# Late residuals on VectorE, a block's last product ahead of the next turn, and a new order of stores in a graph-attention kernel

## The chip, the cores and the metric

The kernel runs on one core of a Trainium2 chip. The core has five engines that work side by side: TensorE (PE) multiplies matrices and transposes, VectorE (DVE) does elementwise work and reductions along a row, ScalarE (ACT) applies functions with a scale and a bias, GpSimd (POOL) does elementwise work in SBUF and issues gathers by index, and SyncE (SP) issues the other transfers. [...] Sixteen DMA engines move the data of all queues. The metric is the time of one execution on the device in microseconds, the lower the better.

## The reference

The computation is one graph-attention layer with a residual and a layer norm, for 4096 nodes with 512 features:

```python
def _L0_gnn_ref(h, adj_mat, W, a):
    ht = (h @ W).reshape(N, N_HEADS, N_HIDDEN).transpose(1, 0, 2)      # 4 heads of 512
    src = jnp.einsum('hnd,hd->hn', ht, a_src)
    dst = jnp.einsum('hnd,hd->hn', ht, a_dst)
    e = jax.nn.leaky_relu(src[:, :, None] + dst[:, None, :], SLOPE) + adj_mat[None]
    att = jax.nn.softmax(e, axis=-1)
    h_prime = jnp.einsum('hij,hjd->hid', att, ht)
    return h_prime.mean(axis=0)
x = _layernorm(x + _L0_gnn_ref(x, adj, L0_gnn_W, L0_gnn_a), axis=-1)
```

The adjacency matrix is 4096 by 4096 float32 (64 MB); its entries are zero or weights up to 1e9. With such weights added to the scores, the softmax of a row is as a rule one at its largest entry and zero elsewhere. The attention output of a row is then one row of x, times the mean of the four heads' weight matrices.

## The kernel before

The kernel uses that fact. For each of the 4096 rows it finds the largest adjacency entry, gathers that one row of x, multiplies it by the mean of the heads' weights, adds x, and normalises. It also proves for every row, with a bound on the scores, that the leading entry wins; rows that fail would be redone by a general branch (`general`, from line 529), which this input skips.

The 4096 rows are 32 blocks (`NB`) of 128 rows. Row `p * 32 + ib` of the matrix is row `p` of block `ib`, so a store of n neighbouring blocks writes n * 2 KB in one run for each of the 128 partitions. `hold` keeps x and later the output of all blocks in SBUF. `Q` is 4, `LATE` is 28 and `BEHIND` is 24. The blocks form three groups:

- Blocks 0 to 23: the residual is added on TensorE, as a product with the identity (`residual`, L221), into the accumulator in PSUM that the four products (`products`, L228) also write; ScalarE takes the statistics and finishes them (`stats`, `finish`) in the main loop. Their stores wait until the loads are queued.
- Blocks 24 to 27: x is not there yet when their products end. ScalarE sets the products aside in SBUF (`put_by`, L241), and x is added after the loop (`add_x`, L244), on GpSimd for 24 to 26 and on VectorE for 27.
- Blocks 28 to 31: x is loaded in time. The residual of 28 and 29 is an identity product on TensorE in the last round, that of 30 an addition on VectorE after its products (L511), and that of 31 two identity products of half a row each (`residual_in_halves`, L266). Most of these blocks take mean and variance on VectorE (`moments`, L281 and L285), the root on ScalarE (L287), the reciprocal (and, with `shift=True`, minus mean times reciprocal) on VectorE (`factor`, L290 and L292), and the ending on VectorE (`normalise`, L297) or ScalarE (`finish`, L261).

For each block the search has two levels. VectorE reduces the 4096 entries of a row to 128 maxima of 32 (`segment_maxima`, L163); `find_segment` takes the largest of them and its place, and GpSimd turns the place into an index and gathers the 32 entries of that segment from the adjacency matrix (L174, L176, L181). Two rounds later `find_column` finds the place within the segment, and GpSimd gathers the row of x (L198, L200, L186). For the last block, `find_column_in_row` searches all 4096 entries on VectorE instead (L206), so that it does not wait for the second gather. TensorE then turns the gathered block (`turn`, L213: four transposes, and a copy by ScalarE, L215) and multiplies.

The order is written out by hand: no scheduler moves anything, and what the main loop (`for t in range(NB)`) and the listing after it (lines 463 to 525) call in turn is each engine's own order. In the loop, round t searches block t, gathers x for block t - 2, multiplies for block t - 3, takes statistics of t - 4. From block 24 on, a block's last product waits until the next block's turn has been issued, so that the turn's copy runs beside it. After the loop come the endings of the last blocks, interleaved with the proof (`bound`, `test`, `count`, `report`).

SyncE issues all loads in the loop; the stores follow behind the last loads: two of four blocks (0 to 3, 4 to 7), eight of two (8 to 23), and at the end, in this order, blocks 28, 29, 24 with 25, 30, 26 with 27, and 31. A store is issued only when its blocks are finished, and those behind it in the list wait with it. Row gathers and segment gathers share GpSimd's queue, whose instructions also include the additions of `add_x` and the final factors of the blocks that ScalarE measures (`rstd`, L255 to L257).

Of the kernel before, what the change touches and what calls it, by code (L numbers as in the profile page):

```python
# [10 lines left out]
U32 = mybir.dt.uint32  # L11
# [55 lines left out]
def leading_rows(ctx, tc, x, adj, W, a, out, ident, v, n_bad, any_bad):  # L67
# [100 lines left out]
    def find_segment(ib):  # L168
        seg = seg_of.pop(ib)
        nc.vector.max(out=top[:, ib, :], in_=seg)  # L170
        at = small.tile([P, 8], U32, name="at")
        nc.vector.max_index(at, top[:, ib, :], seg)  # L172
        row = small.tile([P, 1], U32, name="row")
        nc.gpsimd.tensor_tensor(row, at[:, 0:1], first[:, ib : ib + 1], op=OP.add)  # L174
        lead = lead_pool.tile([P, E], F32, name="lead")
        nc.gpsimd.indirect_dma_start(  # L176
            out=lead, out_offset=None, in_=adj_segs,
            in_offset=bass.IndirectOffsetOnAxis(ap=row[:, :1], axis=0),
        )
        start = at_of[ib] = small.tile([P, 1], U32, name="start")  # L180
        nc.gpsimd.tensor_tensor(start, at[:, 0:1], width, op=OP.mult)  # L181
        lead_of[ib] = lead

# [33 lines left out]
    def residual(ib):  # L217
        start = ib not in o_ps
        if start:
            o_ps[ib] = psum.tile([P, D], F32, name="o")  # L220
        nc.tensor.matmul(o_ps[ib], ident, hold[:, ib, :], start=start, stop=False)  # L221
# [40 lines left out]

    def residual_in_halves(ib):
        o_ps[ib] = [psum.tile([P, D // 2], F32, name="o") for _ in range(2)]
        for k, o in enumerate(o_ps[ib]):
            nc.tensor.matmul(o, ident, hold[:, ib, ts(k, D // 2)], start=True, stop=False)  # L266
# [22 lines left out]
    def factor(ib, shift=False):  # L289
        nc.vector.reciprocal(rt[ib], rt[ib])  # L290
        if shift:
            nc.vector.scalar_tensor_tensor(  # L292
                nm[:, ib : ib + 1], mean_var[ib][:, 0:1], -1.0, rt[ib], op0=OP.mult, op1=OP.mult
            )
# [111 lines left out]
    COLUMN, PROJECT, STATS, FINISH = 2, 3, 4, 6  # L406

    for t in range(NB):
# [30 lines left out]
        if t == NB - 1:  # L439
            for late in range(LATE, NB):  # L440
                row_norm(late)
            residual(LATE)
            residual(LATE + 1)
# [21 lines left out]
    for ib in range(0, 2 * Q, Q):  # L465
        store(nc.sync, ib, Q)
    for ib in range(2 * Q, BEHIND, 2):
        store(nc.sync, ib, 2)
    find_column(NB - 2)
    add_x(nc.gpsimd, BEHIND)  # L470
    add_x(nc.gpsimd, BEHIND + 1)
    find_column_in_row(NB - 1)
    add_x(nc.gpsimd, BEHIND + 2)
    products(LATE, KB - 1, KB)
    residual_in_halves(NB - 1)
    turn(NB - 3)
    products(NB - 3, 0, KB - 1)
    moments(LATE)
    for ib in range(BEHIND, NB):
        find_inner(ib)  # L480
    bound(0)
    products(NB - 3, KB - 1, KB)
    stats(BEHIND)
    factor(LATE)
    normalise(LATE, o_ps.pop(LATE))
    bound(1)
    turn(NB - 2)
    bound(2)
    add_x(nc.vector, LATE - 1)
    stats(BEHIND + 1)  # L490
    moments(LATE - 1)
    products(NB - 2, 0, 2)
    bound(3)
    test()
    pg = count()
    products(NB - 2, 2, KB - 1)
    stats(BEHIND + 2)
    rstd(slice(BEHIND, BEHIND + 2))
    rstd(slice(BEHIND + 2, BEHIND + 3))
    moments(NB - 3)  # L500
    report(pg)
    turn(NB - 1)
# [4 lines left out]
    finish(BEHIND + 1)  # L507
    products(NB - 2, KB - 1, KB)
    products_of_half(NB - 1, 0)
    products_of_half(NB - 1, 1)  # L510
    nc.vector.tensor_add(hold[:, NB - 2, :], o_ps[NB - 2], hold[:, NB - 2, :])  # L511
    o_ps[NB - 2] = hold[:, NB - 2, :]
# [4 lines left out]
    finish(BEHIND + 2)  # L517
    finish(BEHIND + 3)
# [4 lines left out]
    for ib, n in ((NB - 4, 1), (NB - 3, 1), (BEHIND, 2), (NB - 2, 1), (BEHIND + 2, 2)):  # L523
        store(nc.sync, ib, n)
# [154 lines left out]
```

## Time and profile before

| quantity | value |
|---|---|
| median of 3 runs | 236.09 us (235.83 to 236.25) |
| the profiled execution's own time | 236.21 us |
| its span, first to last instruction | 234.6 us |
| granted TensorE clock, mean | 0.975 |
| busy: TensorE / VectorE / ScalarE / GpSimd | 83% / 80% / 48% / 43% |
| bytes moved by DMA | 97.21 MB, mean 414 GB/s |
| of these, read and written in HBM | 88.62 MB and 8.39 MB |
| SyncE's queue / GpSimd's queue | 88.08 MB / 8.92 MB |

The profile is one execution. A line of it names the engine, the line of the kernel, the operation, what it writes and reads, the count, the duration, and the idle time ahead of it with what ended that idle time. `L228` is line 228. A float32 product shows as two records on TensorE. The times in the lists of instructions are microseconds from the first instruction of the program. The DMA share is the mean over the 16 DMA engines.

### The profile page before, as it was taken

The page shows a single profiled execution, that of the slowest core. Times are in us where ns is not written, and L with a number is a line of the kernel's source. Part 1 is how long each engine was busy: PE and PEld are TensorE (multiplying, and loading weights), DVE is VectorE, ACT ScalarE, POOL GpSimd, SP SyncE. Part 2 cuts the span into 40 slices and gives each one's busy share as a digit, 9 for nine tenths or more (in the row PEclk, how much of TensorE's full clock was granted, in tenths as well). Part 3 has the DMA queues.
Part 4 walks back from the last instruction along what each step waited for, and adds up shares of the span by engine and source line. Part 5 has one row for each costly group of instructions (what it writes and reads, how often), then busy time and mean ns, then how long its engine had stood idle before and what let it go on. Part 6 is the DMA issues. An engine that isn't in the chain of part 4 may idle for free.

```text
span 234.6 us, 2498 instructions
## 1 busy us (share of the span) xinstructions
PE 195.2 (83%) x683; PEld 101.4 (43%) x683; DVE 188.4 (80%) x302; ACT 111.6 (48%) x267; POOL 101.2 (43%) x215
## 2 busy tenths in 40 slices
PE   0188929999999999999979879797998968698990
PEld 0034514756565655555534333242443423244460
DVE  1736875589869995999589989998799999989672
ACT  2012011255474747474758354646464645166582
POOL 1012232414527462646353645464365464549130
PEclk9999977999999999999999999999799999999998
DMA  6999999999999999999999999999999999999985
GB/s 226 439 428 426 443 425 430 415 440 412 440 420 426 424 437 434 425 424 428 427 432 433 425 433 422 432 418 429 425 432 418 422 425 427 411 425 419 417 355 210
DMA packets 13697, 97.21 MB, mean 414 GB/s; under 512 B 2152, under 2 KB 2664, under 8 KB 7792
## 3 DMA queue, kind: packets, MB, share of 16 engines
q1 hardware_dynamic: 10080, 88.08, 88.9%
q0 software_dynamic: 3584, 8.92, 9.6%
q8 instruction: 6, 0.10, 0.2%
q14 instruction: 11, 0.09, 0.1%
q10 hardware_dynamic: 16, 0.02, 0.0%
HBM read 88.62 MB, written 8.39 MB: 414 GB/s over the span
## 4 chain that ended last, share of the span: by engine, by line
DMA 45%; POOL 17%; issue 15%; PE 10%; DVE 9%; ACT 1%; POOLq 0%; SPq 0%; DVEq 0%
DMA adj_t<-in_adj_dram 42%; DVE seg L163 8%; PE o L228 7%; POOL lead L176 6%; POOL y L186 5%; DMA y<-in_x_dram,col 3%; POOL sd L256 2%; PE o L270 2%; POOL start L181 1%; POOL row L174 1%; POOL col L200 1%; PE tp L213 1%; PE o L221 1%; ACT yt L215 1%; POOL sd L255 1%
## 5 line engine op out<-in xcount | busy, mean ns | idle before, releaser
L163 DVE TENSOR_REDUCE seg<-adj_t 128x64 f32<-128x2048 f32 (+1 forms) x68 | 146.0, 2149 | 32.7 <-DMA adj_t<-in_adj_dram 32.3
L228 PE MATMUL o<-w_sum,yt 128*128 128x512 f32 x248 | 115.1, 605 | 1.7 <-ACT yt L215 1.7
L228 PEld LDWEIGHTS o<-w_sum,yt 128*128 128x128 f32 x248 | 44.5, 191 | 54.8 <-issue 42.3
L215 ACT COPY yt<-tp 128x512 f32<-128x512 f32 x32 | 18.8, 588 | 44.3 <-PE tp L213 44.3
L176 POOL DMA_INDIRECT lead<-in_adj_dram,row x32 | 32.3, 1010 | 15.5 <-POOL row L174 15.0
L186 POOL DMA_INDIRECT y<-in_x_dram,col x32 | 30.9, 965 | 15.4 <-POOL col L200 15.2
L318 PE MATMUL o<-hold,ident 128*128 128x512 f32 x32 | 18.9, 745 | 17.5 <-DMA hold<-in_L_gnn_W_dram 17.5
L213 PE MATMUL tp<-ident,y 128*128 128x128 f32 x128 | 20.0, 280 | 12.6 <-DMA y<-in_x_dram,col 12.6
L221 PE MATMUL o<-hold,ident 128*128 128x512 f32 x52 | 27.3, 611 | 0.0
L213 PEld LDWEIGHTS tp<-ident,y 128*128 128x128 f32 x128 | 14.9, 143 | 25.4 <-issue 25.0
L174 POOL TENSOR_TENSOR row<-at,first 128x1 uint32<-128x1 uint32 x32 | 6.1, 190 | 42.0 <-DVE at L172 42.0
L336 ACT COPY wt<-tp 128x512 f32<-128x512 f32 x16 | 9.2, 587 | 31.4 <-PE tp L334 31.4
L200 POOL TENSOR_TENSOR col<-start,within 128x1 uint32<-128x1 uint32 x31 | 5.9, 190 | 40.1 <-DVE within L198 40.1
L235 ACT ACTIVATE sq<-hold 128x512 f32<-128x512 f32 x32 | 19.8, 619 | 0.0
L342 PEld LDWEIGHTS pv<-at_d,wt 128*128 128x128 f32 x128 | 16.3, 191 | 6.8 <-ACT wt L336 4.0
L318 PEld LDWEIGHTS o<-hold,ident 128*128 128x128 f32 x32 | 7.4, 243 | 26.7 <-POOL row L174 11.0
L319 ACT ACTIVATE w_sum<-o 128x512 f32<-128x512 f32 x4 | 2.4, 598 | 33.9 <-PE o L318 33.9
L261 ACT ACTIVATE hold<-o,nm,sd 128x512 f32<-128x512 f32 x24 | 17.2, 771 | 0.0
L252 ACT ACTIVATE sq<-o,nm 128x512 f32<-128x512 f32 x24 | 16.5, 688 | 0.8
L342 PE MATMUL pv<-at_d,wt 128*128 128x2 f32 x128 | 15.3, 244 | 0.6 <-ACT wt L336 0.6
L250 ACT ACTIVATE sq<-o 128x512 f32<-128x512 f32 x24 | 14.6, 609 | 0.0
L334 PEld LDWEIGHTS tp<-ident,hold 128*128 128x128 f32 x64 | 7.9, 142 | 6.9 <-issue 6.9
(85 smaller groups left out, 139.8 us busy)
## 6 DMA issues: line engine op xcount, KB each, us to landing
adj_t<-in_adj_dram SPq DMA_DIRECT2D x27, 2048.0 KB, 31.3
hold<-in_x_dram SPq DMA_DIRECT2D x7, 1024.0 KB, 33.2
adj_t<-in_adj_dram SPq DMA_DIRECT2D x6, 1024.0 KB, 25.7
out_dram<-hold SPq DMA_DIRECT2D x10, 512.0 KB, 15.2
adj_t<-in_adj_dram SPq DMA_DIRECT2D x8, 512.0 KB
hold<-in_L_gnn_W_dram SPq DMA_DIRECT2D x4, 1024.0 KB
out_dram<-hold SPq DMA_DIRECT2D x2, 1024.0 KB
hold<-in_x_dram SPq DMA_DIRECT2D x2, 512.0 KB, 14.1
```

The lines of the kernel that those rows point to most:

```text
L163: nc.vector.tensor_reduce(seg_of[ib][:, ts(k, S // n)], adj_t[ib][:, ts(k, N // n)].rearrange("p (s e) -> p s e", e=E), axis=AX.X, op=OP.max,)
L176: nc.gpsimd.indirect_dma_start(out=lead, out_offset=None, in_=adj_segs, in_offset=bass.IndirectOffsetOnAxis(ap=row[:, :1], axis=0),)
L186: nc.gpsimd.indirect_dma_start(out=y, out_offset=None, in_=x, in_offset=bass.IndirectOffsetOnAxis(ap=col[:, :1], axis=0),)
L213: nc.tensor.transpose(tp[:, kb, :], y[:, ts(kb, P)], ident)
L215: nc.scalar.copy(yt, tp)
L221: nc.tensor.matmul(o_ps[ib], ident, hold[:, ib, :], start=start, stop=False)
L228: nc.tensor.matmul(o_ps[ib], yt_of[ib][:, kb, :], w_sum[:, kb, :], start=(start and kb == 0), stop=(kb == KB - 1),)
L235: nc.scalar.activation(sq, hold[:, ib, :], AF.Square, accum_out=xx[:, ib : ib + 1])
L252: nc.scalar.activation(sq, o, AF.Square, bias=nm[:, i], accum_out=sd[:, i])
L261: nc.scalar.activation(hold[:, ib, :], o_ps.pop(ib), AF.Identity, bias=nm[:, i], scale=sd[:, i])
L318: nc.tensor.matmul(o, ident, hold[:, w_at + kb * H + h, :], start=(h == 0), stop=(h == H - 1))
L342: nc.tensor.matmul(pv[:, kb, h : 2 * H : H], wt[:, k, :], at_d[:, k, h : 2 * H : H], start=(k == 0), stop=(k == KB - 1),)
```

## The change

Five edits, nearly all in what follows the last loads.

1. The identity products of blocks 28 and 29 are gone. Instead `add_residual` adds x on VectorE once the products are complete, as block 30 already had it; block 28's ending moves from VectorE to ScalarE, with the shift that it needs.
2. In `factor` the shift is a one-input operation with the reciprocal as a scalar, where it was a two-input operation.
3. Block 29's work is issued in another order: its turn now follows the last product of block 28 and stands ahead of block 31's residual halves; its own last product stands ahead of the turn of block 30, and three products of block 30 stand together ahead of the turn of 31, which comes before the moments of 29.
4. GpSimd: the second half of `find_segment` is a function of its own, `fetch_segment`; for block 31 it is called after block 30's row gather. Before block 31's row gather stands the addition of x for block 24 alone; those of 27, 25 and 26 follow it, 27's moved here from VectorE. The endings of 26 and 27 move from ScalarE to GpSimd (`finish_on_chip`).
5. SyncE: the stores of 0 to 23 go in the order `HELD`, with the two four-block stores third and sixth; the last six go as 28, 24 with 25, 26 with 27, 29, 30, 31.

```diff
     def find_segment(ib):
         seg = seg_of.pop(ib)
         nc.vector.max(out=top[:, ib, :], in_=seg)
-        at = small.tile([P, 8], U32, name="at")
+        at = at_of[ib] = small.tile([P, 8], U32, name="at")
         nc.vector.max_index(at, top[:, ib, :], seg)
+        if ib < NB - 1:
+            fetch_segment(ib)
+
+    def fetch_segment(ib):
+        at = at_of.pop(ib)
         row = small.tile([P, 1], U32, name="row")
...
-        start = at_of[ib] = small.tile([P, 1], U32, name="start")
-        nc.gpsimd.tensor_tensor(start, at[:, 0:1], width, op=OP.mult)
         lead_of[ib] = lead
+        if ib < NB - 1:
+            start = at_of[ib] = small.tile([P, 1], U32, name="start")
+            nc.gpsimd.tensor_tensor(start, at[:, 0:1], width, op=OP.mult)
...
+    def finish_on_chip(ib):
+        i, h = slice(ib, ib + 1), hold[:, ib, :]
+        o_ps.pop(ib)
+        nc.gpsimd.tensor_scalar(h, h, sd[:, i], nm[:, i], op0=OP.mult, op1=OP.add)
+
+    def add_residual(ib):
+        nc.vector.tensor_add(hold[:, ib, :], o_ps[ib], hold[:, ib, :])
+        o_ps[ib] = hold[:, ib, :]
...
         if shift:
-            nc.vector.scalar_tensor_tensor(
-                nm[:, ib : ib + 1], mean_var[ib][:, 0:1], -1.0, rt[ib], op0=OP.mult, op1=OP.mult
+            nc.vector.tensor_scalar(
+                nm[:, ib : ib + 1], mean_var[ib][:, 0:1], rt[ib], -1.0, op0=OP.mult, op1=OP.mult
             )
...
+    HELD = ((8, 2), (10, 2), (0, Q), (12, 2), (14, 2), (Q, Q), (16, 2), (18, 2), (20, 2), (22, 2))
...
                 row_norm(late)
-            residual(LATE)
-            residual(LATE + 1)
...
-    for ib in range(0, 2 * Q, Q):
-        store(nc.sync, ib, Q)
-    for ib in range(2 * Q, BEHIND, 2):
-        store(nc.sync, ib, 2)
+    for ib, n in HELD:
+        store(nc.sync, ib, n)
     find_column(NB - 2)
+    fetch_segment(NB - 1)
     add_x(nc.gpsimd, BEHIND)
-    add_x(nc.gpsimd, BEHIND + 1)
     find_column_in_row(NB - 1)
-    add_x(nc.gpsimd, BEHIND + 2)
+    for ib in (LATE - 1, BEHIND + 1, BEHIND + 2):
+        add_x(nc.gpsimd, ib)
     products(LATE, KB - 1, KB)
+    turn(NB - 3)
     residual_in_halves(NB - 1)
-    turn(NB - 3)
     products(NB - 3, 0, KB - 1)
+    bound(0)
+    stats(BEHIND)
+    add_residual(LATE)
     moments(LATE)
+    bound(1)
+    factor(LATE, shift=True)
     for ib in range(BEHIND, NB):
         find_inner(ib)
-    bound(0)
     products(NB - 3, KB - 1, KB)
-    stats(BEHIND)
-    factor(LATE)
-    normalise(LATE, o_ps.pop(LATE))
-    bound(1)
     turn(NB - 2)
+    finish(LATE)
+    moments(LATE - 1)
+    stats(BEHIND + 1)
     bound(2)
-    add_x(nc.vector, LATE - 1)
-    stats(BEHIND + 1)
-    moments(LATE - 1)
-    products(NB - 2, 0, 2)
     bound(3)
     test()
+    products(NB - 2, 0, KB - 1)
     pg = count()
-    products(NB - 2, 2, KB - 1)
     stats(BEHIND + 2)
     rstd(slice(BEHIND, BEHIND + 2))
     rstd(slice(BEHIND + 2, BEHIND + 3))
+    add_residual(NB - 3)
+    turn(NB - 1)
     moments(NB - 3)
     report(pg)
-    turn(NB - 1)
     factor(LATE - 1, shift=True)
     factor(NB - 3)
     normalise(NB - 3, o_ps.pop(NB - 3))
     finish(BEHIND)
     finish(BEHIND + 1)
+    finish_on_chip(BEHIND + 2)
+    finish_on_chip(BEHIND + 3)
     products(NB - 2, KB - 1, KB)
     products_of_half(NB - 1, 0)
     products_of_half(NB - 1, 1)
-    nc.vector.tensor_add(hold[:, NB - 2, :], o_ps[NB - 2], hold[:, NB - 2, :])
-    o_ps[NB - 2] = hold[:, NB - 2, :]
+    add_residual(NB - 2)
     moments(NB - 2)
     stats_of_half(NB - 1, 0)
     factor(NB - 2)
     normalise(NB - 2, o_ps.pop(NB - 2))
-    finish(BEHIND + 2)
-    finish(BEHIND + 3)
     stats_of_half(NB - 1, 1)
     moments(NB - 1)
     factor(NB - 1, shift=True)
     finish_in_halves(NB - 1)
-    for ib, n in ((NB - 4, 1), (NB - 3, 1), (BEHIND, 2), (NB - 2, 1), (BEHIND + 2, 2)):
+    for ib, n in ((LATE, 1), (BEHIND, 2), (BEHIND + 2, 2), (NB - 3, 1), (NB - 2, 1)):
         store(nc.sync, ib, n)
     store(nc.sync, NB - 1, 1)
```

## The prediction

> **What bounds the kernel now.** I read the page first, then the instructions in order of time for the last 35 us of each engine, then short stretches of the last 10 us for the DMA engines. All times below are on the profiled execution's clock: span 234.6 us, its own time 236.21 us, so 1.6 us lie outside the span; the median of the runs shown is 236.09 us, 0.12 us below it.
>
> The page's row of bytes a second (40 slices) and its sum:
>
> ```profile
> GB/s 226 439 428 426 443 425 430 415 440 412 440 420 426 424 437 434 425 424 428 427 432 433 425 433 422 432 418 429 425 432 418 422 425 427 411 425 419 417 355 210
> DMA packets 13697, 97.21 MB, mean 414 GB/s; under 512 B 2152, under 2 KB 2664, under 8 KB 7792
> ```
>
> From the second slice to the third from the end the 16 DMA engines are full. Nothing of the change touches the bytes. Only the last two slices (some 11.7 us) have room. In them TensorE is the busy engine. Its instructions in order of time:
>
> ```profile
> 203.58 0.63 PE L213 MATMUL tp<-ident,y 128*128 128x128 f32 x4 [1.84 <-DMA y<-in_x_dram,col]
> ...
> 207.61 1.88 PE L221 MATMUL o<-hold,ident 128*128 128x512 f32 x4
> ...
> 216.28 2.84 PE L228 MATMUL o<-w_sum,yt 128*128 128x512 f32 x6 [0.68 <-ACT yt L215]
> ...
> 221.21 1.99 PE L228 MATMUL o<-w_sum,yt 128*128 128x512 f32 x4 [0.37 <-ACT yt L215]
> ...
> 225.53 3.70 PE L270 MATMUL o<-w_sum,yt 128*128 128x256 f32 x16
> ```
>
> TensorE last waits for a gather at 203.58 and then runs to 229.2 with two holes, 0.68 and 0.37 us. Behind it stands block 31's ending, and then the last store:
>
> ```profile
> 229.27 0.43 DVE L304 BATCH_NORM_STATS2 halves_st<-o 128x6 f32<-128x256 f32 x1 [0.65 <-PE o L270]
> ...
> 230.69 0.56 ACT L310 ACTIVATE hold<-o,nm,sd 128x256 f32<-128x256 f32 x1 [0.42 <-DVE nm L292]
> ```
>
> So compute ends at 231.25, the last store is issued at 231.3 and lands 2.3 us later (233.6), the span closes 1.0 us after. A TensorE shortened by 2 us would seem to move the end by 2 us. The short stretches speak against it (after the colon: length; per engine busy; at the end TensorE's clock, DMA share, GB/s):
>
> ```profile
> 227.40:227.70 0.30, 0.30 (x3) 0.27 (x2) 0.16 (x1) 0.30 (x2) 0.00 (x0) 1.00 0.25 96
> 227.70:229.00 1.30, 1.30 (x8) 1.00 (x6) 0.88 (x3) 1.30 (x2) 0.00 (x0) 1.00 0.99 391
> ...
> 231.30:231.50 0.20, 0.00 (x0) 0.00 (x0) 0.00 (x0) 0.00 (x0) 0.00 (x0) 1.00 0.28 103
> 231.50:231.70 0.20, 0.00 (x0) 0.00 (x0) 0.00 (x0) 0.00 (x0) 0.00 (x0) 1.00 0.15 61
> 231.70:231.90 0.20, 0.00 (x0) 0.00 (x0) 0.00 (x0) 0.00 (x0) 0.00 (x0) 1.00 0.10 41
> 231.90:232.10 0.20, 0.00 (x0) 0.00 (x0) 0.00 (x0) 0.00 (x0) 0.00 (x0) 1.00 0.05 20
> 232.10:232.90 0.80, 0.00 (x0) 0.00 (x0) 0.00 (x0) 0.00 (x0) 0.00 (x0) 1.00 0.87 328
> ```
>
> Sixteen engines: 0.05 is one engine. When the last store's data begins (232.1), one engine is only just done with the store before it; between 227.4 and 227.7, where the others starve, four engines (0.25 of 16) still have a backlog. I read this as one lagging engine that never starved: it would not finish earlier if stores came earlier.
>
> [...] the page's instruction queues (17 packets, 0.19 MB) agree, and such packets are uneven load, a possible cause of the lag. [...] the trace has the two-input add (L244) at 1.28 us and no wide one-input operation on GpSimd. [...]
>
> **The change, part by part.**
>
> *Residuals of 28 and 29.* Two identity products go: 1.72 us by the chain of waits. VectorE gets two additions from PSUM at 0.69 us (L511's row). 28's ending moves from VectorE (0.81, L297 from PSUM) to ScalarE (0.77, L261), and 29's reads SBUF: 0.55 instead of 0.81.
>
> *28's last product, the turn of 29, 31's residual halves.* The halves (0.86 us) now stand behind the turn and cover ScalarE's copy: the 0.68 us hole goes. The sum on TensorE: 1.72 + 0.68 = 2.4 us to be had, if the gathers come. The chain has a gather at 7.3 us from issue to landing (196.17 to 203.44); turns in 209 to 225 did not wait, so others were no slower; I take 6.3, with 5.8 (the segment gather's landing) and 7.3 as ends.
>
> *Gathers.* GpSimd before:
>
> ```profile
> 210.41 0.97 POOL L176 DMA_INDIRECT lead<-in_adj_dram,row x1 [0.51 <-PE tp L213]
> ...
> 212.99 2.50 POOL L244 TENSOR_TENSOR hold<-hold,adj_t 128x512 f32<-128x512 f32 x2
> 215.65 0.96 POOL L186 DMA_INDIRECT y<-in_x_dram,col x1 [0.16 <-PE tp L213]
> ```
>
> Block 31's segment gather (row, gather, multiply: 1.9 us) now stands behind block 30's row gather, which moves from 212.0 to about 210.8. One addition, not two, stands before 31's row gather: 215.65 becomes 215.0, held by VectorE's 4.4 us search (ends 214.8). The additions of 27, 25, 26 follow, 216.0 to 219.8. What is late instead: 31's segment, issued 212.5, landing 218.3; VectorE wants it at 218.2, so at most some 0.5 us.
>
> *TensorE, step by step.* Turn 28 at 207.8 (its gather, issued 201.5, is there by 207.8); four products at 0.88 to 212.4; turn 29 waits for its gather (206.05 + 6.3 = 212.4; 213.3 at worst); halves 0.86; four products and a small transpose to 217.5; turn 30 (gather 210.8 + 6.3 = 217.1) to 218.0; copy 0.6 on ScalarE; three products to 221.3; turn 31 (215.0 + 6.3 = 221.3); its copy queues on ScalarE behind two statistics passes of 1.56 us, the second ending at 222.8, so it ends at 223.4; halves of 31, 3.6 us, to 227.0. Before: 229.2.
>
> *VectorE's tail.* 29's residual and moments 220.5 to 222.1, report to 222.6, factors; normalise 29 after its root (ScalarE, 223.7) 224.0 to 224.5; 30's addition and moments to 226.1; first half, normalise 30 to 227.4; second half then. It equals TensorE's end, so the two are level. From the second half to the last store is 2.0 us as before: 229.5 instead of 231.3, a gain of 1.8 us. [...]
>
> *Finishing 26 and 27 on GpSimd.* From 224.0, two passes. [...] above: 1.28 us, the add's row. I take 1.0: pair done by 226.2. It takes 1.6 us from ScalarE, none of it on the path.
>
> *Shift with one input.* 0.16 us either way, two instructions[...].
>
> *Stores.* Same sizes and number. The 4-block stores now go third and sixth: row gathers meet smaller packets, worth some tenths to gathers, at worst nothing. The last stores' order on SyncE's queue is 28 (219.4 instead of 217.5; the backlog covers it), pair 24 (225.3), pair 26 (226.3), 29, 30, 31. SyncE issues in order: 29 and 30, ready by 224.5 and 227.4, stand behind both pairs.
>
> *The end.* From 224.5 the shares times lengths sum to 6.6 us of work for the mean engine: fed without holes and evenly spread, data would end at 231.1 instead of 233.0. The lagging engine has 232.1 plus the last store's 0.7 (0.26 MB at 415 GB/s is 0.63): 232.8 to 233.0. Its gain is 0 to 0.3 us. I take 0.3: **235.8 us**.
>
> **Rivals.**
>
> *A, the lagging engine binds (0.60):* gain 0 to 0.5, 235.6 to 236.1. For it: the 0.05 share. Against: that it is one and the same engine is inferred.
>
> *B, the compute gain comes through (0.22):* the lag is an accident of one instruction fetch and falls elsewhere. Then the end follows the last store's issue, 1.8 us earlier at most, and even data ends 1.9 us earlier: 234.3[...]. For it: in two-microsecond stretches from 226 to 232 the mean share is 0.74 to 0.79.
>
> *C, slower (0.18):* SyncE's queue stands at pair 26 until GpSimd is done, with five blocks (1.31 MB, 3.2 us) behind that issue; with 0.8 us to start and 0.5 to land, landing is 4.5 us after it. Before it was 233.6, so it decides from an issue at 229.1, that is 2.5 us a pass. At 3 us a pass: 230.1, landing 234.6, **237.1 us**. Against: both ends of the estimate lie below half of that; for it: the operation is not in the trace [...].
>
> *D, nothing is done:* the gathers land late and TensorE waits the 2.4 us away. Also ends at 236.1; counted with A.
>
> **How the numbers follow.** A measurement of this kernel can tell some 0.2% (0.47 us). A: faster 0.13, same 0.46, slower 0.01. B: all faster. C: slower 0.15, same 0.03. Sums: 0.35, 0.49, 0.16. Range 234.8 to 236.6: it holds A, most of B, and C's mild half; A alone is 235.5 to 236.2.
>
> **What would show it.** No L221 after 206; turn 29 before 213; TensorE's end near 227; GpSimd's passes near 1 us; the last store issued near 229.5. For A: DMA share near 1 to about 231.5, then a tail of 0.05 to 0.2 before the end, and the last landing over 3 us after its issue. For B: landing at 2.3 us. The prediction is wrong if the share falls evenly, or if SyncE waits at pair 26 beyond 229.

## The result, and the profile after

The changed kernel takes 236.06 us (median of 22 runs, 235.36 to 239.19) beside 236.19 us of the kernel before on the same chip (22 runs, 235.68 to 238.01): a ratio of 1.0009 with the 95% interval 0.9985 to 1.0033. That is no difference that can be told. The ratio is not the quotient of the two medians: it leaves out one slow run of the changed kernel, the one of 239.19 us. The forecast was 235.8 us with the range 234.8 to 236.6 and "same" as the likeliest sign. So the number was right. The reasons were right only in part, and it took some luck for the number to hold.

The profiled execution of the changed kernel took 238.12 us, 2 us more than its median: 9 of the 22 runs were above 236.9 us. So a second profile of the same kernel (236.47 us, span 234.9 us) is read beside it.

TensorE first. These are its instructions in order of time in the first profile after the change (start, length, engine, line, in brackets the idle time ahead and what ended it):

```profile
209.85 1.09 PE L219 MATMUL tp<-ident,y 128*128 128x128 f32 x4 [2.46 <-DMA y<-in_x_dram,col]
210.73 5.69 PE L234 MATMUL o<-w_sum,yt 128*128 128x512 f32 x10
216.25 0.60 PE L219 MATMUL tp<-ident,y 128*128 128x128 f32 x4
...
226.74 3.72 PE L285 MATMUL o<-w_sum,yt 128*128 128x256 f32 x16
```

and in the second:

```profile
207.66 0.63 PE L219 MATMUL tp<-ident,y 128*128 128x128 f32 x4 [0.99 <-DMA y<-in_x_dram,col]
208.13 4.54 PE L234 MATMUL o<-w_sum,yt 128*128 128x512 f32 x10
213.54 0.63 PE L219 MATMUL tp<-ident,y 128*128 128x128 f32 x4 [0.87 <-DMA y<-in_x_dram,col]
...
219.49 0.63 PE L219 MATMUL tp<-ident,y 128*128 128x128 f32 x4 [0.84 <-DMA y<-in_x_dram,col]
...
225.08 3.72 PE L285 MATMUL o<-w_sum,yt 128*128 128x256 f32 x16
```

The identity products of 28 and 29 are gone, and no hole of 0.68 us stands ahead of block 29's products. But TensorE now waits for gathers. In the second profile three turns wait 0.99 + 0.87 + 0.84 = 2.70 us, which is more than the 2.4 us that the change saved. TensorE ends at 228.8 (225.08 + 3.72), 0.4 us earlier than in the profile before. But that profile had lost 1.84 us to block 27's gather (at 203.58), where this one lost 0.64. In two more profiles of the order before (of the runs below with one late addition and with the new store order) TensorE ends at 228.8 and 229.0. So TensorE as a whole gained nothing.

The three waits have different reasons. The trace has the landing of a gather on each of the 16 DMA engines. Block 28's gather was there 5.9 us after its issue; TensorE simply came to it early, at 206.7. Block 29's took 7.25 us. Block 30's took 8.1 us, but 15 of the 16 engines had landed by 217.95, before TensorE asked for it at 218.65. The last landed at 219.36, and the turn started at 219.49. A packet of 16 KB on an instruction queue (the profile's kind `instruction`) had started at 217.32; that it stood on the same engine is inferred from the times here and below, since the trace doesn't number the engines.

In the first profile, the turn of 28 alone waits 2.46 us, and then ten products take 5.69 us where they take 4.54 in the second. In three stretches of that profile (length; busy per engine; at the end TensorE's clock, the DMA share, GB/s):

```profile
207.30:209.80 2.50, 0.09 (x1) 0.00 (x0) 2.04 (x3) 0.45 (x2) 0.57 (x1) 1.00 1.03 416
209.80:213.20 3.40, 3.35 (x7) 1.90 (x8) 2.37 (x7) 1.11 (x3) 0.82 (x2) 0.50 1.03 426
213.20:216.00 2.80, 2.80 (x8) 1.28 (x7) 2.80 (x1) 2.52 (x9) 2.48 (x4) 1.00 1.02 421
```

The clock is halved for the 3.4 us after the hole, and TensorE ends at 230.5, 1.2 us later than before. That the turns waited is what rival D said; that the gathers were late holds for only some of the waits.

The second thing to read is the end, which the prediction looked at only through the last store. The program closes with a drain on each engine. First the kernel before, then the changed one (instructions of the closing line; count, shortest, middle and longest length in ns, first and last start in us):

```profile
L674 POOLq DRAIN  x3: 40/103/5306, 228.2 to 234.3; - x3
L674 SPq DRAIN  x3: 7/7/7, 233.7 to 234.0; - x3
```

```profile
L686 POOLq DRAIN  x3: 40/103/5306, 230.4 to 236.3; - x3
L686 SPq DRAIN  x3: 7/7/7, 235.2 to 236.0; - x3
```

SyncE's first drain starts when its wait for the last store is over. GpSimd's first drain is the long one, 5.306 us. Before, SyncE stood at 233.7 and GpSimd's drain ended at 228.2 + 5.3 = 233.5: two ends, 0.2 us apart. After, they are 235.2 and 230.4 + 5.3 = 235.7: GpSimd is the last. The span closes some 0.8 to 1.0 us after the later of the two, in every profile here. Over the runs (us from the first instruction; "drain over" is the start plus 5.3, from the trace):

| kernel | TensorE ends | last store issued | SyncE's wait over | GpSimd's drain over | span |
|---|---|---|---|---|---|
| before | 229.2 | 231.3 | 233.7 | 233.5 | 234.6 |
| after, first profile | 230.5 | 232.6 | 235.2 | 235.7 | 236.6 |
| after, second profile | 228.8 | 230.9 | 233.6 | 234.1 | 234.9 |
| after, GpSimd's factors elsewhere | 230.0 | 232.1 | 236.1 | 233.4 | 237.0 |
| before, one late GpSimd addition | 228.8 | 230.9 | 233.3 | 236.2 | 237.0 |
| before, GpSimd's factors elsewhere | 229.6 | 231.7 | 234.8 | 232.5 | 235.7 |
| after, products back | 229.3 | 231.4 | 233.7 | 233.9 | 234.7 |
| mixed order | 228.9 | 231.0 | 234.4 | 232.7 | 235.3 |
| mixed order, one store less | 229.0 | 231.2 | 234.3 | 232.9 | 235.2 |
| before, new store order | 229.0 | 231.1 | 233.4 | 233.3 | 234.3 |
| after, turns without gathers | 228.0 | 230.2 | 233.0 | 233.3 | 234.2 |
| before, turns without gathers | 228.3 | 230.4 | 233.5 | 232.6 | 234.4 |
| mixed, turns without gathers | 228.2 | 230.3 | 233.7 | 232.0 | 234.5 |
| after, turns without gathers, old segment place | 226.7 | 228.8 | 233.7 | 232.0 | 234.6 |

Why GpSimd is later after the change: its last instructions and its load of the closing flag, before and after.

```profile
225.25 0.19 POOL L257 TENSOR_TENSOR nm<-nm,sd 128x1 f32<-128x1 f32 x1
```

```profile
L61 POOLq TENSOR_LOAD <-any_bad x1: 508/508/508, 225.2 to 225.2; - x1
```

```profile
227.20 0.19 POOL L263 TENSOR_TENSOR nm<-nm,sd 128x1 f32<-128x1 f32 x1
227.50 1.56 POOL L272 TENSOR_SCALAR hold<-hold,sd,nm 128x512 f32<-128x512 f32 x2
```

```profile
L61 POOLq TENSOR_LOAD <-any_bad x1: 508/508/508, 227.4 to 227.4; - x1
```

From the start of this load to the drain's end it is 8.3 us in both. The last factor starts 1.95 us later than before, since ScalarE's statistics of block 26, on which it waits, come later. The two endings of 0.78 us stand behind the factor, but the load starts ahead of them and runs beside them. Measured from the factor's start, the load comes only some 0.3 us later than before; that is all the endings cost the close. In the second profile the factor starts at 225.54 and the load at 225.78: 0.3 us from the factor and 0.3 us from the endings.

### The profile page after: what moved, and what is told of

It reads as the page before. It is cut to its first block, busy times and chain, and to the rows that moved or that the text cites. A ratio compares the mean times of both kernels' runs of the same rounds, so it can differ in the third digit from the quotient of the medians.

```text
span 236.6 us, 2490 instructions
## 1 busy us (share of the span) xinstructions
PE 195.0 (82%) x679; PEld 101.1 (43%) x679; DVE 188.2 (80%) x303; ACT 110.8 (47%) x266; POOL 103.5 (44%) x217
## 4 chain that ended last, share of the span: by engine, by line
DMA 36%; issue 23%; POOL 23%; PE 8%; DVE 6%; ACT 1%; SPq 1%; POOLq 0%; DVEq 0%
DMA adj_t<-in_adj_dram 29%; POOL lead L181 8%; POOL y L192 7%; PE o L234 5%; DVE seg L163 5%; DMA lead<-in_adj_dram,row 3%; DMA y<-in_x_dram,col 3%; POOL sd L262 2%; POOL row L179 2%; POOL start L188 2%; PE o L285 2%; POOL col L206 1%; PE tp L219 1%; POOL sd L261 1%; SPq L118 1%
## 5 line engine op out<-in xcount | busy, mean ns | idle before, releaser
L234 PE MATMUL o<-w_sum,yt 128*128 128x512 f32 x248 | 117.0, 614 | 1.0 <-ACT yt L221 1.0
L234 PEld LDWEIGHTS o<-w_sum,yt 128*128 128x128 f32 x248 | 45.4, 195 | 55.5 <-issue 43.7
L221 ACT COPY yt<-tp 128x512 f32<-128x512 f32 x32 | 18.8, 587 | 43.7 <-PE tp L219 40.8
L333 PE MATMUL o<-hold,ident 128*128 128x512 f32 x32 | 18.8, 741 | 18.2 <-DMA hold<-in_L_gnn_W_dram 18.2
L227 PE MATMUL o<-hold,ident 128*128 128x512 f32 x48 | 24.8, 598 | 0.0
```

The source lines that it names most:

```text
L221: nc.scalar.copy(yt, tp)
L234: nc.tensor.matmul(o_ps[ib], yt_of[ib][:, kb, :], w_sum[:, kb, :], start=(start and kb == 0), stop=(kb == KB - 1),)
L333: nc.tensor.matmul(o, ident, hold[:, w_at + kb * H + h, :], start=(h == 0), stop=(h == H - 1))
```

## The experiments

The theory at the start: TensorE's gain is eaten by gathers that take 7 us, not 6.3, and the end is set by whichever of GpSimd's close and the last store is later. The rivals: the prediction's case A (a lagging DMA engine sets the end whatever compute does), and that one of the other edits costs what TensorE gains.

### The changed kernel once more

> The changed kernel itself, unchanged, for a second profile. Three theories. Lag (the prediction's): one DMA engine with a backlog sets the end; then the last store lands more than 3 us after its issue. End of GpSimd: GpSimd closes its program with a drain of 5.3 us (seen in both profiles), and the span ends some 9.1 us after its last instructions are issued; then the drain ends after SyncE's last wait, as in the first profile of the changed kernel (235.75 against 235.22), and about 9.1 us lie between GpSimd's load of the flag and the end. Hole: TensorE waits over 1 us for block 28's gather, since the two residual products no longer stand there, and its clock drops for 3.4 us; then the hole is there again. Time 235.6 to 236.4, or about 2 us more where an instruction fetch delays the gather.

Measured: 236.49 us (20 runs, 235.65 to 238.24), before 236.03 us, ratio 1.0021 (1.0003 to 1.0038). By the two intervals the change gains no more than 0.15% and loses no more than 0.4%. Its profile is the second one above. The gathers of 29, 30 and 31 landed 7.25, 8.1 and 7.1 us after their issue; in the kernel before it was 6.84, 6.45 and 7.09. The 8.1 us hold the packet of 16 KB; without it, by the other 15 engines, it was 6.7.

### One late addition on GpSimd, in the kernel before

> The kernel before with one GpSimd operation of one element per row added, 0.2 us long, that waits for block 30's reciprocal (at 228.0) and that nobody reads. End of GpSimd: its flag load moves from 225.2 to 228.0 or so, the drain ends near 236.3, and the kernel is slower by 2.4 to 2.9 us, though the operation is off every path of data. Lag: no change, since no byte and no store moves.

```diff
+    tick = small.tile([P, 1], F32, name="tick")
+    nc.gpsimd.tensor_tensor(tick, rt[NB - 2], rt[NB - 2], op=OP.add)
     finish(BEHIND + 2)
     finish(BEHIND + 3)
```

An addition of 128 numbers that nobody reads, placed so that it must wait for block 30's reciprocal.

```profile
227.69 0.19 POOL L518 TENSOR_TENSOR tick<-sd 128x1 f32<-128x1 f32 x1 [2.67 <-DVE sd L290]
```

```profile
L676 POOLq DRAIN  x3: 40/103/5306, 230.9 to 236.8; - x3
L676 SPq DRAIN  x3: 7/7/7, 233.3 to 236.5; - x3
```

Measured: 238.98 us, ratio 1.0147 (1.0105 to 1.0189). The last store was done at 233.3, earlier than before the edit; GpSimd's drain ended at 230.9 + 5.3 = 236.2, and the span followed it to 237.0. So 0.19 us of work whose result nobody reads cost 2.9 us in the medians (238.98 to 236.03). This shows that GpSimd's last instruction is a second end of the program.

### GpSimd's last work taken away, in both kernels

> The changed kernel with GpSimd's late work taken away: the factors of blocks 24 to 26 come from ScalarE's root and two small VectorE operations, and 26 and 27 are finished on ScalarE again. GpSimd's last instruction is then the addition of x for block 26, some 5 us earlier. End of GpSimd: the drain ends before 232 and no longer binds, the end follows SyncE's last store; a gain of 0.3 to 1.0 us against the changed kernel. Lag: no change within 0.3 us. Hole: the hole at block 28 stays and costs what it cost.

> The kernel before with the factors of blocks 24 to 26 taken from GpSimd (ScalarE's root, two VectorE operations). End of GpSimd: the drain ends before 230; but SyncE's own last wait was only 0.2 us behind the drain, so the gain is 0 to 0.2 us, within the noise. Lag: no change. If the kernel before becomes slower by over 0.5 us, the added VectorE work is on its path.

```diff
-    rstd(slice(BEHIND, BEHIND + 2))
-    rstd(slice(BEHIND + 2, BEHIND + 3))
+    late_root(slice(BEHIND, BEHIND + 3))        # root on ScalarE
...
+    late_factor(slice(BEHIND, BEHIND + 3))      # reciprocal and product on VectorE
     factor(LATE - 1, shift=True)
...
-    finish_on_chip(BEHIND + 2)                  # in the changed kernel
-    finish_on_chip(BEHIND + 3)                  # these two went back to ScalarE
```

Measured: the changed kernel 237.78 us, ratio 1.0074 (1.0054 to 1.0095); the kernel before 236.59 us, ratio 1.0019 (1.0009 to 1.0029). GpSimd's drain was over at 233.4 and 232.5, out of the way, but the last store now ended at 236.1 and 234.8. One root for three blocks waits for the third block's statistics, so the stores of both pairs came late and in a bunch: in the changed kernel the last four issues lie between 230.5 and 232.1. The profile of the changed kernel also had the hole of 2.45 us ahead of turn 28, with half clock for 3.4 us behind it. Against the forecasts (a gain of 0.3 to 1.0 us, and of 0 to 0.2) both runs are misses; whether the added VectorE work, which the second expectation named, made the kernel before 0.56 us slower was not taken apart. The edit moved the limit from one end to the other, and says nothing for or against GpSimd as the limit of the changed kernel.

### The identity products of 28 and 29 put back

> The changed kernel with one part undone: the residuals of blocks 28 and 29 are identity products on TensorE again, ahead of the turn of 28 (1.72 us), and VectorE's two additions are gone. Hole: the products stand where TensorE would wait for block 28's gather (1.0 us in the second look, 2.45 us where an instruction fetch hits that gather, with the clock halved for 3.4 us after); so no clock drop after 207, TensorE's end no later than in the second look by over 0.5 us though it has 1.72 us more work, and the executions above 237 us, 5 of 20 in the second look and 9 of 22 before that, go: median 235.9 to 236.2. Lag: no change in the median. If the taken products had been a gain on the path, this is 1 us or more slower than the changed kernel.

```diff
                 row_norm(late)
+            residual(LATE)
+            residual(LATE + 1)
...
-    add_residual(LATE)
...
-    add_residual(NB - 3)
```

Measured: 236.22 us, ratio 1.0011 (0.9989 to 1.0034). TensorE does 1.72 us more and ends at 229.3, between the two profiles of the changed kernel. Its turns of 28, 29, 30 and 31 wait for no gather; the work put back fills the time. The same number with and without the 1.72 us is what theory and rival D say of TensorE. That the executions of over 236.9 us would go with it was not so: 4 of 12.

### The new store order alone, in the kernel before

> The kernel before with one part of the change alone: the stores of 0 to 23 in the new order. All theories: no change within 0.2%. The gathers of 29, 30 and 31, which took 6.8 to 7.1, 6.5 and 6.8 to 7.1 us from issue to landing with the old order, and 7.0 to 7.3, 6.7 to 7.0 and 6.3 to 7.1 us with the new one in the changed kernel, stay within 0.5 us of these.

```diff
-    for ib in range(0, 2 * Q, Q):
-        store(nc.sync, ib, Q)
-    for ib in range(2 * Q, BEHIND, 2):
-        store(nc.sync, ib, 2)
+    for ib, n in HELD:
+        store(nc.sync, ib, n)
```

Measured: 235.97 us, ratio 0.9997 (0.9978 to 1.0017). This edit alone has no effect on the time, but it has one on the gathers. Block 30's gather took 7.28 us here and 6.45 in the kernel before. In the seven profiles of this study with the old store order it took 6.25 to 6.47 us, in the seven with the new order 6.58 to 7.28, and 8.1 with the instruction packet. The DMA packets between 216 and 220 us, when this gather is under way, before and here:

```profile
DMA packets 471, 1.68 MB, mean 419 GB/s; under 512 B 62, under 2 KB 62, under 8 KB 471
```

```profile
DMA packets 348, 1.70 MB, mean 426 GB/s; under 512 B 47, under 2 KB 47, under 8 KB 233
```

In the kernel before every packet of these 4 us is under 8 KB; here 348 - 233 = 115 are not, in the time of the second four-block store. The longer gather is shown by this run. That the larger packets are the reason fits, but they weren't varied on their own. In this kernel TensorE comes to turn 30 just late enough not to wait.

### A mixed order

> A mixture: residuals of 28 and 29 on TensorE, each in front of a turn that waits for its gather; the stores of 0 to 23 in the order of the kernel before; of the change: the turn of 29 ahead of 31's residual halves, the gather of 30 ahead of 31's segment gather, three products of 30 together. New: x is added to 25 and 26 ahead of 27, ScalarE takes the statistics of 25 and 26 as soon as they are there (25 near 218, 26 near 221), the endings of 24 to 27 are on ScalarE, 24 with 25 near 224. End of GpSimd: its last instruction is issued near 224 instead of 225.2, the drain ends near 232.5 and no longer binds. Lag: the end stays within 0.3 us of the kernel before. If what binds is when the first of the last stores is issued, the time of the last one, and GpSimd's end, all three come earlier here: 235.2 to 235.6, 0.4 to 0.8 us less than before.

```diff
             row_norm(late)
+            residual(LATE)
...
-    for ib, n in HELD:
-        store(nc.sync, ib, n)
+    for ib in range(0, 2 * Q, Q):
+        store(nc.sync, ib, Q)
+    for ib in range(2 * Q, BEHIND, 2):
+        store(nc.sync, ib, 2)
...
+    residual(NB - 3)
     turn(NB - 3)
...
+    rstd(slice(BEHIND, BEHIND + 2))             # ahead of test(), statistics of 25 and 26 ahead of it
+    rstd(slice(BEHIND + 2, BEHIND + 3))
...
-    finish_on_chip(BEHIND + 2)
-    finish_on_chip(BEHIND + 3)
+    finish(BEHIND + 2)
+    finish(BEHIND + 3)
...
-    for ib, n in ((LATE, 1), (BEHIND, 2), (BEHIND + 2, 2), (NB - 3, 1), (NB - 2, 1)):
+    for ib, n in ((LATE, 1), (BEHIND, 2), (NB - 3, 1), (BEHIND + 2, 2), (NB - 2, 1)):
```

Measured: 236.70 us, ratio 1.0023 (1.0011 to 1.0035), where 235.2 to 235.6 was expected. GpSimd is done at 232.7, the last store is issued at 231.0, 0.3 us earlier than in the kernel before, and yet it ends 0.7 us later. The short stretches of its end (as above; the last two numbers are the DMA share and GB/s):

```profile
231.80:232.20 0.40, 0.00 (x0) 0.00 (x0) 0.00 (x0) 0.00 (x0) 0.00 (x0) 0.50 0.81 317
232.20:232.60 0.40, 0.00 (x0) 0.00 (x0) 0.00 (x0) 0.00 (x0) 0.00 (x0) 0.50 0.77 297
232.60:233.00 0.40, 0.00 (x0) 0.00 (x0) 0.00 (x0) 0.00 (x0) 0.00 (x0) 0.50 0.14 20
...
233.40:233.80 0.40, 0.00 (x0) 0.00 (x0) 0.00 (x0) 0.00 (x0) 0.00 (x0) 0.50 0.12 46
```

From 232.6 on only two of the 16 DMA engines work (0.12 to 0.14), and from 232.6 to 233.0 they move next to nothing. The trace has two packets of 8 KB on an instruction queue there, at 232.46 and 232.50; the last store's packets on two engines ran from 232.77 to 233.83, when those on the other 14 had ended by 232.6. In the kernel before, the two packets came at 232.98 and 233.01, behind nearly all of the store.

### The mixed order with one store less

> The mixture without the store of blocks 26 and 27 (0.52 MB of the output are not written). Lag, or bytes of the last stores as the bound: the end comes up to 1.2 us earlier than in the mixture. Compute as the bound (the last store's issue and 2.0 to 2.3 us), or GpSimd's end: no change within 0.3 us.

```diff
-    for ib, n in ((LATE, 1), (BEHIND, 2), (NB - 3, 1), (BEHIND + 2, 2), (NB - 2, 1)):
+    for ib, n in ((LATE, 1), (BEHIND, 2), (NB - 3, 1), (NB - 2, 1)):
```

Measured: 236.85 us in one run; the last store issued at 231.15, done on most engines by 233.1 and on two by 234.2. With 0.52 MB less to write the end is the same, which by its expectation speaks against a bound by the bytes of the last stores in this order. It is a single run. The two late engines again go with instruction packets, at 232.12 and 232.79; the place of these packets in time was read, not varied.

### Turns that wait for no gather

The next three take TensorE's waits away without touching the transfers: the turns of the last four blocks read x, which is there, and the gathers are still issued and moved.

> The changed kernel with the turns of blocks 28 to 31 reading x of the same block, which is in SBUF long before, in place of the gathered rows; the gathers are still issued and moved, nothing on TensorE waits for them. The output of those four blocks is therefore another one. Theory 1 (the gathers took TensorE's gain back, and the end follows compute once they don't): TensorE ends at 226 to 227.5 instead of 228.8 to 230.5, the last store is issued by 229.7, GpSimd's closing flag load starts by 224.8 because ScalarE's statistics come earlier, and the median is 234.6 to 235.4 us, at least 0.7 us below the kernel before. Theory 2 (the prediction's case A: the DMA engines' backlog sets the end, whatever TensorE does): TensorE ends as early, but the last store lands over 3 us after its issue and the median stays at 235.7 to 236.3 us.

> The kernel before with the same substitution (the turns of blocks 28 to 31 read x, the gathers are still moved). Both theories: of the turns after block 28's none waited for a gather before, so TensorE gains at most some tenths to 1 us (only block 28's turn can start sooner) and the median is 235.5 to 236.2 us. If this kernel gains as much as the changed one with the same substitution, the gathers are no reason for the change's missing gain.

> The mixed order (two residuals still on TensorE, statistics of 25 and 26 early, blocks 24 to 27 finished on ScalarE) with the same substitution. Theory 1: TensorE ends near 227, GpSimd's flag load starts by 224.4, the last store is issued by 230.0, and the median is 234.8 to 235.6 us, unless the two instruction fetches after the closing branches of VectorE and ScalarE hold up the last store again, which gives 235.8 to 236.6 us. Theory 2: 235.8 to 236.6 us with a late landing and no such fetch.

```diff
-            nc.tensor.transpose(tp[:, kb, :], y[:, ts(kb, P)], ident)
+            nc.tensor.transpose(tp[:, kb, :], (y if ib < LATE else hold[:, ib, :])[:, ts(kb, P)], ident)
```

Measured: the changed kernel 235.80 us (19 runs, 235.45 to 236.26), ratio 0.9983 (0.9966 to 1.0000); the kernel before 235.82 us, ratio 0.9993 (0.9979 to 1.0007); the mixed order 236.18 us, ratio 1.0018 (1.0007 to 1.0028). Theory 1 asked for at least 0.7 us from the changed kernel and is wrong in that. The time, 235.8, is what theory 2 gave, but not its sign: the last store landed 2.8 us after its issue, not over 3, and GpSimd's close was the later end (233.3 beside 233.0). The kernel before gains as much from the same substitution, 0.14 us in the medians beside 0.16. By the expectation above, the gathers alone then don't explain the missing gain: with them out of the way, something else keeps both kernels at the same time. The mixed order's 236.18 lies within the forecasts of both theories.

Not one of the 19 runs of the changed kernel lies above 236.9 us now, where 15 of 42 did in the two earlier sets (9 of 22 and 6 of 20). This fits long executions that come from TensorE's waits, but it doesn't show it: 3 of the 20 runs of the mixed order without such waits lie above 236.9 us too, and so did 4 of the 12 with the products back and 4 of the 22 of the kernel before. In the changed kernel, TensorE ends only at 228.0, for a new reason:

```profile
219.55 0.20 DVE L198 MAX8 inner<-lead 128x8 f32<-128x32 f32 x1 [1.19 <-DMA lead<-in_adj_dram,row]
```

```profile
221.80 0.22 PE L409 MATMUL px<-gap,ones 128*1 128x32 f32 x2 [1.09 <-DVE gap L405]
...
224.32 3.72 PE L285 MATMUL o<-w_sum,yt 128*128 128x256 f32 x16 [0.85 <-ACT yt L221]
```

Block 31's segment gather, which the change moved behind block 30's row gather (issued 213.1), lands at 219.5; VectorE waits 1.19 us for it. The place alone is not the reason. The three profiles of the mixed order have the same place and the old store order, and there this gather took 5.25 to 5.31 us; in the five with this place and the new store order it took 5.8 to 7.1. Behind that stand the moments of 27, for which ScalarE waits 2.03 us with its statistics and the copy of turn 31 queued behind, and the proof's test, for which TensorE waits 1.09 us; it then waits 0.85 us for the copy.

### The same, with the segment gather at its old place

> The changed kernel with the turns of blocks 28 to 31 reading x (as in the run before), and block 31's segment gather issued where the kernel before issues it, ahead of block 30's row gather (another output for those four blocks, as there). Without TensorE's waits for row gathers, VectorE waited 1.19 us for that segment, and behind it stood block 27's moments, ScalarE's root and statistics, the copy of turn 31 and GpSimd's factors. Theory 1 (that segment is the next limit, and both ends hang on it): the segment lands by 218, VectorE's wait is gone, GpSimd's flag load starts by 224.2 instead of 225.0, the last store is issued by 229.4 instead of 230.2, and the median falls to 234.9 to 235.4 us. Theory 2 (a backlog of the DMA engines sets the end): the issue moves as far, but the last landing stays at 232.8 or later and the median at 235.6 to 236.0 us.

```diff
     def find_segment(ib):
...
-        if ib < NB - 1:
-            fetch_segment(ib)
+        fetch_segment(ib)
...
     find_column(NB - 2)
-    fetch_segment(NB - 1)
```

Measured: 236.20 us (12 runs), before 235.92 us, ratio 1.0001 (0.9988 to 1.0014). This is far from the 234.9 to 235.4 of theory 1 and 0.2 us above the range of theory 2. It is the clearest run of the study. The segment landed by 216.0, VectorE's wait for it is gone, and all of compute came forward. TensorE's last instructions, the last store's landing (shortest, middle and longest time from issue to landing of a store), and the drains:

```profile
222.99 3.72 PE L284 MATMUL o<-w_sum,yt 128*128 128x256 f32 x16
```

```profile
DMA to landing us min/median/max: 4.8/12.1/15.3
```

```profile
L684 POOLq DRAIN  x3: 40/103/5306, 226.7 to 234.4; - x3
L684 SPq DRAIN  x3: 7/7/7, 233.7 to 234.1; - x3
```

TensorE ends at 226.7, 2.5 us before the kernel before; the last store is issued at 228.8, also 2.5 us earlier; GpSimd's drain is over at 232.0. The last store lands at 233.7, as before: it takes 4.8 us, where it took 2.3. Its end in stretches:

```profile
228.80:229.40 0.60, 0.00 (x0) 0.00 (x0) 0.00 (x0) 0.00 (x0) 0.00 (x0) 1.00 0.98 389
229.40:229.80 0.40, 0.00 (x0) 0.00 (x0) 0.00 (x0) 0.00 (x0) 0.00 (x0) 1.00 0.80 312
...
231.60:231.80 0.20, 0.00 (x0) 0.00 (x0) 0.00 (x0) 0.00 (x0) 0.00 (x0) 0.50 0.13 51
...
232.80:233.20 0.40, 0.00 (x0) 0.00 (x0) 0.00 (x0) 0.00 (x0) 0.00 (x0) 0.50 0.05 20
```

Every engine of the core is idle, and the DMA share falls from 0.98 over 0.13 (two engines) to 0.05 (one). The trace has the landings of the last store on the 16 engines: six by 230.8, six more by 231.7, three by 232.3, the last at 233.7. The store before it spreads from 229.6 to 232.6, and one that was issued at 207.8 already from 219.4 to 222.9. So the engines carry backlogs that differ by 3 us, and do so for 14 us. The share times length from 228.8 to 233.2 is 2.3 us of work for the mean engine: evenly spread it would have ended at 231.1. The last engine also took an instruction packet at 231.9, which took 0.31 us and with the slow packets behind it cost some 0.7 us (an estimate from their times). Without it this landing would have come at 233.0 (233.7 less the 0.7), still only 0.6 us before the 233.6 of the kernel before, with compute 2.5 us earlier.

## Why the prediction was right, step by step

- **Residuals, holes, products.** Right: L221 (now L227) is not seen after 206, the 0.68 us hole is gone, the 0.37 us hole stays. The 2.4 us "to be had, if the gathers come" is a sound sum. They did not all come.
- **"I take 6.3" for a row gather.** This step failed. Block 29's gather took 6.84 us in the kernel before and 7.04 and 7.25 in the two profiles of the changed one; block 30's took 6.45 before, then 7.03 and 8.1; block 31's 6.4 to 7.1. The argument was that turns between 209 and 225 had not waited before, so their gathers were no slower than the one of 7.3 us. But a turn that doesn't wait tells only that the data came before the turn, and the turns were late. The 7.3 us were themselves an accident: block 27's gather had landed on 15 of 16 engines after 6.1 us, and the last was late behind a packet of 16 KB at 201.21. TensorE missed its forecast end by 1.8 us in the second profile. Of these, 1.1 us are turn 29 (213.54 instead of 212.4, for the slower gather) and 0.84 us are turn 30 (for the packet of 16 KB). "Turn 29 before 213" was named as a sign, and it failed in both profiles (213.54 and 216.25). The wait of 0.99 us ahead of turn 28 was no lateness of the gather. So rival D, counted with A, is what happened to TensorE, for reasons that it named only in part.
- **Stores of four blocks third and sixth, "worth some tenths to gathers, at worst nothing".** The wrong sign for two of them. The new order lengthens block 30's gather by 0.8 us (7.28 beside 6.45, in the run with this edit alone) and goes with a later segment of block 31. Whether the changed kernel with the old store order would be faster was not tried.
- **Turn 28 "is there by 207.8".** Right in the second profile (the turn starts at 207.66; TensorE, with a shorter hole at block 27, was there 0.99 us earlier). In the first the gather took 7.3 us, one of 16 DMA engines 1.3 us behind the rest, right after a packet of 16 KB on an instruction queue, at 206.59. The prediction named such packets as a possible cause of a lag among the stores; that they hit a gather was not foreseen. Without the two identity products ahead of the turn nothing covers such a hit: 2.46 us of waiting and the halved clock, and 2.45 us and the same clock in the run with GpSimd's factors elsewhere. In the kernel before with the late addition the same packet came at the same stage, and the turn waited 0.73 us.
- **TensorE near 227, last store issued near 229.5.** Measured 228.8 and 230.9 in the second profile, 230.5 and 232.6 in the first. Wrong for the two reasons above, and right once neither the row gathers nor the late segment hold it up: 226.7 and 228.8.
- **The segment gather.** Forecast 218.3 and "at most some 0.5 us" for VectorE; it landed at 219.5 (with TensorE's waits taken away) and cost VectorE 1.19 us, and in the second profile 0.74 us. The forecast took 5.8 us from issue to landing; with the new store order it was 6.4 in that run, with the old one at the same place 5.25 to 5.31.
- **Finishing on GpSimd, 1.0 us a pass.** Measured 0.78 us. The 1.0 us was an estimate of the author's, with the 1.28 us of the two-input addition as its upper end. Rival C, which needed 2.5 us a pass, is out: SyncE did wait for the pair (issued at 227.4 and 229.1, forecast 226.3) but mostly since the factors came late: the pair began at 225.84 in the second profile, not at 224.0. In the first profile this lies just past the 229 that the prediction had named as a sign of being wrong; the last store was not held up by it, as it waited for block 31.
- **Shift with one input, "0.16 us either way".** Measured 0.21 against 0.16: slower by 0.05 us, in three places of which block 31's is on the path.
- **Case A, the lagging engine.** Right as a limit, not as what bound the changed kernel. In its own two profiles the DMA engines ran dry after 226 (a share of 0.54 from 226 to 228 in the second), the backlogs evened out, and the last store landed 2.5 and 2.6 us after its issue, not over 3 as the sign for A asked. Only when compute is really earlier does the limit show, and then just as forecast: a share near 1, a tail of 0.05 to 0.2, a landing over 3 us after the issue. The prediction's 231.1 for evenly spread data is what the stretches of that run also sum to. What it left open, whether it is "one and the same engine", the trace can't tell. That the spread lasts for 14 us speaks for it, and so does the kernel before: of six stores that landed between 222.9 and 228.5, each one's last engine came 1.0 to 1.1 us after its last but one.
- **Missed altogether: GpSimd's close.** No step of the prediction looked at what follows GpSimd's last instruction. The two endings moved to GpSimd got a time for each pass and no cost at the end. They (some 0.3 us) and the later factors made GpSimd's drain the last event of the changed kernel in both profiles (235.7 against 235.2, 234.1 against 233.6), some 0.5 us by the traces; no run takes this away from the changed kernel and leaves the rest as it was. It pulled the same way as the gathers. That the number held is therefore in part luck: 235.8 was worked out from case A, and other ends, sized too small or at nothing, took the gain before A could.

So the gain was stopped three times over: by the turns' waits for gathers, behind them by GpSimd's close, and behind that by the uneven backlog of the DMA engines. By the last run the backlog alone would have held the gain to some 0.6 us (the estimate above), and the 12 executions of that run show no gain at all.

## What to carry to other kernels

When several ends stand within half a microsecond of each other (233.7 and 233.5 here), list all of them with their times before costing an edit: the last store, but also each engine's own close. A wait that doesn't appear in a trace bounds a transfer's latency only from the side of the consumer's time; when the consumer is to come earlier, take the latency from the landing times of transfers of that kind, on each DMA engine: one late engine of 16 may be an accident (block 27's gather: 1.2 us behind the rest), most of them late is the latency. When stores change places, ask which gathers will be under way beside the large ones (block 30's: 7.28 us instead of 6.45). And where the DMA engines are full, ask whether the end follows the last issue or the engine with the longest backlog: make the compute free (other data, same transfers) and see if the end moves.

## What the runs showed of the hardware

- GpSimd closes this program with a drain of 5.306 us, the same in all profiles; from its load of the closing flag (225.2 in the kernel before) to the drain's end it was 8.3 to 8.6 us. An addition of 0.19 us at 227.7 cost 2.9 us in this way.
- An instruction packet of 16 KB took 0.88 to 1.94 us of a DMA engine and falls at another time in each execution (one of them between 201.2 and 217.3); in 13 of the 14 profiles one of the late row gathers landed 1.2 to 1.5 us later on one engine than on all others, after such a packet. Two of 8 KB started 1.6 us after the closing branches of VectorE and ScalarE in the kernel before (branches at 231.4), and 1.7 and 1.4 us after them in the first profile of the changed one (232.6 and 233.1). In the mixed order two such packets started before the last store's packets on two engines, and it ended there 1.2 us after the others.
- Block 30's gather of 128 rows took 6.25 to 6.47 us in the seven profiles without packets of 8 KB between 216 and 220 us, and 6.58 to 7.28 in the six with them in which no instruction packet hit it (8.1 in the seventh).
- Holes of 2.46 and 2.45 us on TensorE were followed by 3.4 us at half clock; the holes of up to 1.95 us in the last 35 us of these profiles were not.
